# A convolution stage split in two: 11 batches ahead of the scans, 21 batches in slices beside them, with the band matrices kept in DRAM

## The chip, the core and the metric

The kernel runs on one core of one Trainium2 chip. The metric is the device time of one execution in microseconds. Engines are called by the profile's names: PE (TensorE matmul), PEld (its weight loads), DVE (VectorE), ACT (ScalarE), POOL (GpSimd), SP (the queue that issues DMAs).

## The reference, cut to what matters

The input is x, float32, 32 batches x 96 channels x 56 x 56. Two layers follow each other.

```python
# layer 0: ConvNeXt block
h = depthwise_conv7x7(x, conv_w, padding=3) + conv_b      # one 7x7 filter per channel
h = layernorm_over_channels(h) * ln_g + ln_b
h = gelu(h @ w1 + b1) @ w2 + b2
x1 = layer_scale * h + x

# layer 1: two Mamba blocks over the 3136 pixels of a batch as a sequence
seq = x1
for i in range(2):
    xs, z = split(layernorm(seq) @ in_w[i])               # 192 channels each
    xc = silu(causal_conv4(xs)); dt, Bm, Cm = split(xc @ xproj_w[i])
    delta = softplus(dt @ dt_w[i] + dt_b[i])
    h[t] = exp(delta*A) * h[t-1] + delta*xc * Bm          # 16 states per channel: a scan over t
    y = sum_states(h * Cm) + D * xc
    seq = seq + (y * silu(z)) @ out_w[i]
out = batchnorm(fuse(seq, pooled(x1))) + x1
```

Only the depthwise 7x7 convolution is placed differently by the change; the computation stays the same.

## The kernel before, in words

**The convolution stage.** The loop at L291 goes over 48 pairs of channels (`p`). A pair's image rows lie on the partitions: 2 channels x 56 rows = 112. The load at L293 brings all 32 batches of the pair into `xpad`, a tile padded by 3 columns on each side; its rows in DRAM are runs of 56 values, 224 bytes. Seven predicated copies on DVE (L298) write the taps of the pair into `band`, seven 112x112 band matrices, one for each horizontal tap. PE multiplies the seven matrices with seven shifted views of `xpad` (L307), 8 batches (448 columns) at a time, four groups per pair, 28 matmuls in all; a float32 matmul is two records in the profile. ACT adds the bias on the way out of PSUM (L311, tile `ct`), and the store at L314 writes the pair into `conv_d` in DRAM. `band` and `xpad` exist three times each. POOL has nothing to do here.

**The scan stages.** After that come 256 stages: 32 batches x 4 chunks of 784 pixels x 2 Mamba layers. The order of instructions is written out by hand (the manual schedule at L873): no scheduler moves anything, and each engine takes its instructions in the order of the Python code. A stage has 24 steps, six groups `j` of 32 channels times four groups `g` of states. A step has one scan on DVE (L798), ahead of it for most groups a product on DVE (L791), and after it one product on POOL (L802). For the groups j = 2 and j = 5 (`POOLED`) the first product is on POOL instead (L775): it reads the tile `us`, loaded by `load_u`, and its instructions lie at steps 0, 2, 4, 6 (j = 2) and 12, 14, 16, 18 (j = 5). `us` has two buffers. PE spreads the values of a group over 128 partitions for the product at L791 (`spread`, L764), at steps 3, 11, 15 and 23, and sums the states three steps behind the scan (`add_up`, matmuls L835 and L829). ACT computes the exponentials (L749) one or two steps ahead.

**The pieces around the scans.** Everything else is cut into pieces that carry a slot, a step number counted from the start of the stage (24 is the start of the next one, -10 is step 14 of the stage before). `run` calls a step's pieces in the order of the fraction. `prep` prepares the next Mamba stage: layer norm, the projections (L521), softplus (L586), and the loads of `bc` (L566), `d4` (L629) and `us` (L620). `post` at slot 7.5 projects the stage before (L682, L688). `block0` runs half a chunk of the ConvNeXt block of the next batch: it loads `cv` from `conv_d` (L379), and its pieces are `center` (PE, L343, slot 11.1), `square` (ACT, L348), `mean` (PE, L353), `root` (ACT, L359 and L360: logarithm and exponential) and `norm` at 14.1, a product on DVE (L405, output `hz`) that is called ahead of the scan of step 14; the MLP follows. The same step has the layer norm pieces of `prep`. PSUM banks `ps0` to `ps2` are single tiles that these pieces share.

**DMA.** All loads and stores go through the SP queue in the order of the code, apart from the output stores at the end. Each DMA takes one of eight completion semaphores in turn, and an issue waits for the DMA that had the same one before.

Of the kernel before, what the change touches and what calls it, by code (L numbers as in the profile page):

```python
# [30 lines left out]
F32 = mybir.dt.float32  # L34
I32 = mybir.dt.int32
AF = mybir.ActivationFunctionType
# [5 lines left out]
H = W = 56  # L42
L = H * W
C = 96
# [6 lines left out]
NCH = 4  # L51
CH = L // NCH
HC = CH // 2
ROWS = HC // W
# [6 lines left out]
def convnext_mamba_kernel(  # L61
# [31 lines left out]
    nc = tc.nc  # L93
    B = x.shape[0]

    dram = ctx.enter_context(tc.tile_pool(name="dram", bufs=1, space=DRAM))
    const = ctx.enter_context(tc.tile_pool(name="const", bufs=1))

    conv_d = dram.tile([C * H, B * W], F32, name="conv_d")
    stats_d = dram.tile([C, B * NCH, 12], F32, name="stats_d")  # L100
    x1_d = [dram.tile([C, L], F32, name=f"x1_d{b}", tag=f"x1_d{b}") for b in range(B)]
    o_d = [dram.tile([C, L], F32, name=f"o_d{b}", tag=f"o_d{b}") for b in range(B)]
# [83 lines left out]
    for i in range(2):  # L186
# [12 lines left out]
        if i == 1:  # L199

            d["res"] = fw1
            for q in range(NQ):
                ps = sups.tile([128, 512], F32, name="ps", tag="nps")
# [5 lines left out]
                ps = sups.tile([128, 512], F32, name="ps", tag="nps")  # L209
# [36 lines left out]


    R2 = 2 * H
    GB = min(8, B)
    with tc.tile_pool(name="cc", bufs=1) as cc, tc.tile_pool(name="cx", bufs=3) as cx, tc.tile_pool(  # L250
        name="cp", bufs=6, space=PSUM
    ) as cps:
        ones = cc.tile([R2, R2], F32, name="ones")
        nc.vector.memset(ones, 1.0)
        masks = []
        for dh in range(7):
            m = cc.tile([R2, R2], F32, name="m", tag="m", bufs=2)
# [13 lines left out]
            mi = cc.tile([R2, R2], I32, name=f"mi{dh}", tag=f"mi{dh}")  # L271
            nc.vector.tensor_copy(mi, m)
            masks.append(mi)
        cw = cc.tile([R2, C // 2, 49], F32, name="cw")
        cb = cc.tile([R2, C // 2], F32, name="cb")
        wv = conv_w.rearrange("(p two) k -> two p k", two=2)
        bv = conv_b.rearrange("(p two) k -> two p k", two=2)
        for j in range(2):
            nc.sync.dma_start(cw[j * H : (j + 1) * H], wv[j].partition_broadcast(H))
            nc.sync.dma_start(  # L280
                cb[j * H : (j + 1) * H].unsqueeze(2), bv[j].partition_broadcast(H)
            )
        bands, xpads = [], []
        for i in range(3):
            t = cc.tile([R2, 7, R2], F32, name=f"band{i}", tag=f"band{i}")
            nc.gpsimd.memset(t, 0.0)
            bands.append(t)
            t = cc.tile([R2, B, W + 6], F32, name=f"xpad{i}", tag=f"xpad{i}")
            nc.gpsimd.memset(t, 0.0)
            xpads.append(t)  # L290
        for p in range(C // 2):  # L291
            xp, T = xpads[p % 3], bands[p % 3]
            nc.sync.dma_start(  # L293
                xp[:, :, 3 : 3 + W],
                x[:, 2 * p : 2 * p + 2, :].rearrange("b c (h w) -> (c h) b w", w=W),
            )
            for dh in range(7):
                nc.vector.copy_predicated(  # L298
                    T,
                    masks[dh].unsqueeze(1).broadcast_to([R2, 7, R2]),  # L300
                    cw[:, p, dh * 7 : (dh + 1) * 7].unsqueeze(2).broadcast_to([R2, 7, R2]),
                )
            ct = cx.tile([R2, B * W], F32, name="ct")
            for gb in range(0, B, GB):
                ps = cps.tile([R2, GB * W], F32, name="ps")
                for dw in range(7):
                    nc.tensor.matmul(  # L307
                        ps, T[:, dw, :], xp[:, gb : gb + GB, dw : dw + W],
                        start=(dw == 0), stop=(dw == 6),
                    )  # L310
                nc.scalar.activation(  # L311
                    ct[:, gb * W : (gb + GB) * W], ps, AF.Identity, bias=cb[:, p : p + 1]
                )
            nc.sync.dma_start(conv_d[p * R2 : (p + 1) * R2, :], ct)  # L314


    with ExitStack() as main:
        wp = main.enter_context(tc.tile_pool(name="wp", bufs=2))
# [5 lines left out]
        def psum(k):  # L324

            return pp.tile([128, 512], F32, name="ps", tag=f"ps{k}", bufs=1)
# [17 lines left out]
            return ps  # L344

        def squared(ps):
            sq = wp.tile([C, HC], F32, name="sq", tag="sq", bufs=3)
            nc.scalar.activation(sq, ps[0:C, 0:HC], AF.Square)  # L348
            return sq

# [20 lines left out]
        def block0(b, c, s):  # L371
            k = c * 2 + s
            v = {}

            def load():
                if k == 0:
                    batch_sums[b] = wp.tile([C, NCH * 2], F32, name="sums", tag="sums", bufs=2)
                v["cv"] = wp.tile([C, ROWS, W], F32, name="cv", tag="cv", bufs=1)
                nc.sync.dma_start(  # L379
                    v["cv"],  # L380
                    conv_d.rearrange("(c h) w -> c h w", h=H)[
                        :, k * ROWS : (k + 1) * ROWS, b * W : (b + 1) * W
                    ],
                )

# [68 lines left out]
            def fuse():  # L454
# [3 lines left out]
                nc.scalar.activation(fb, ps[0:C, 0:1], AF.Identity, bias=fusb)  # L458
                batch_bias[b] = fb

            last = [(21.5, total), (33.3, pool), (34.3, fuse)] if k == 2 * NCH - 1 else []
            return last + [
                (-6, load), (2, load_x), (11.1, center), (12.1, square), (12.4, mean),
                (12.8, root), (14.1, True, norm), (15.6, up), (15.9, gelu), (17.3, down),
                (18.3, residual),
            ]


# [6 lines left out]
        def prep(S):  # L475

            i, b, c = S.i, S.b, S.c
            d = lay[i]
            v = {}
# [135 lines left out]

            def load_u(k):
                def piece():
                    t = wp.tile([128, CH], F32, name="us", tag="us", bufs=2)
                    for s in range(4):
                        nc.sync.dma_start(t[32 * s : 32 * s + 32], v["uu"][k])  # L620
                    S.us[POOLED[k]] = t

                return piece

            def load_d4(j):
                def piece():
# [14 lines left out]
            t = (-7.6, -7.5, -6.5, -6, 0, 0.1, 1, 2.3, 3.1, 3.4, 4)  # L641
# [7 lines left out]
            elif S is stages[3]:  # L649
# [17 lines left out]
                (max(18.3, t[10] + 3.1), store_u(0)), (25.2, product(2)), (26.3, store_u(1)),  # L667
                (max(17, t[10] + 2), load_d4(0)), (max(18, t[10] + 3), load_d4(1)),
                (max(20, t[10] + 3.2), load_u(0)), (23, load_d4(2)),
                (26, load_d4(3)), (28.9, load_u(1)), (30, load_d4(4)), (35, load_d4(5)),  # L670
            ]

        def post(S):
# [55 lines left out]
        for i, b, c in order:  # L729
            S = Stage()  # L730
            S.i, S.b, S.c, S.d, S.da, S.e = i, b, c, lay[i], {}, {}
            stages.append(S)
        halfs = [(b, c, s) for b in range(1, B) for c in range(NCH) for s in range(2)]

        def wide():
# [107 lines left out]
        def put(m, pieces):  # L843
            for slot, *piece in pieces:
                where = slots if len(piece) == 1 else within
                where.setdefault(m * NSTEP + math.floor(slot), []).append((slot % 1, piece[-1]))
# [14 lines left out]
        for m, S in enumerate(stages):  # L861
            if m:
                put(m, post(stages[m - 1]))
            for j in POOLED:
                put(m, [(NG * (j - 2) + 2 * g, pooled(m, j, g)) for g in range(NG)])
            if 2 <= m < len(halfs) + 2:
                put(m, block0(*halfs[m - 2]))
            if m + 1 < len(stages):
                put(m, prep(stages[m + 1]))
        put(len(stages), post(stages[-1]))  # L870
# [116 lines left out]
```

## Time and profile before

| what | value |
|---|---|
| median of 3 runs | 18194.72 us (18187.29 to 18194.83) |
| profiled execution, device time | 18182.61 us |
| its span, first to last instruction | 18180.9 us |
| convolution stage, first to last matmul of L307 | 97.8 to 1120.4 us |
| batch 0 of the ConvNeXt block and the first preparation | 1120 to about 1307 us |
| scan stages, first to last scan of L798 | 1307 to 17804 us, 64.4 us a stage (16497 / 256) |
| final batch norm and output | to the end |

The profiled execution lies 12 us below the median. The spans in the table are starts of instructions in the trace.

How to read the page: busy time of an engine is the time in which at least one of its instructions runs. In a list of groups, a line gives the code line, the engine, the operation, the tiles written and read, their shapes, the count, the busy time in us, the mean duration in ns, and the idle time ahead of them with what ended it. In the timeline a line gives start, duration, engine, line and operation; merged instructions carry a count. PEclk is the clock granted to PE as a share of full speed.

### The profile page before, as it was taken

Reading aid. Unit: us, or ns where it says so; the run is one execution under the profiler, and the core shown is the slowest. Engines: PE = TensorE matmul, PEld = TensorE weight load, DVE = VectorE, ACT = ScalarE, POOL = GpSimd, SP = SyncE. Lnnn points to the kernel's source line nnn. Section 1 sums busy time; section 2 is a strip of 40 time slices with the busy share of each in tenths; the row PEclk is TensorE's granted clock in tenths of the full one; section 3 lists DMA queues with packets and bytes.
Section 4 is the critical chain, followed back from the end, with each engine's and each line's share of the span. In section 5 each row is a group of like instructions: output and inputs, shape, how many; then the busy total and the mean of one; then the engine's idle time right before and its main releaser. Section 6 shows DMA issues by size and latency. Waiting matters only on the chain. (4 is left out here: it accounts for less than half of the span.)

```text
span 18180.9 us, 209835 instructions
## 1 busy us (share of the span) xinstructions
PE 15482.2 (85%) x65304; PEld 5247.5 (29%) x65304; DVE 16188.3 (89%) x12591; ACT 11251.4 (62%) x17431; POOL 15631.6 (86%) x8993
## 2 busy tenths in 40 slices
PE   8988888888888888888888888888888888888871
PEld 3432222222222222222222222222222222222220
DVE  3329999999999999999999999999999999999994
ACT  0136666666666666666666666666666666666652
POOL 0019999999999999999999999999999999999991
PEclk9989999999999999999999999999999999999985
DMA  3324555555555555555555555555555555555548
GB/s 69 75 70 120 128 126 126 127 126 126 124 127 125 129 126 129 124 129 125 126 126 126 127 126 127 124 127 124 128 125 129 126 129 124 129 125 127 126 110 271
DMA packets 1358198, 2279.26 MB, mean 125 GB/s; under 512 B 619974, under 2 KB 751346, under 8 KB 1357076
## 3 DMA queue, kind: packets, MB, share of 16 engines
q1 hardware_dynamic: 1349908, 2227.31, 49.6%
q10 hardware_dynamic: 7168, 38.54, 0.6%
q8 instruction: 515, 8.44, 0.2%
q14 instruction: 607, 4.97, 0.1%
HBM read 1878.92 MB, written 385.94 MB: 125 GB/s over the span
## 5 line engine op out<-in xcount | busy, mean ns | idle before, releaser
L802 POOL TENSOR_TENSOR da<-h,bc 128x784 f32<-128x784 f32 x6144 | 11268.8, 1855 | 901.2 <-DVE h L798 860.7
L798 DVE TENSOR_TENSOR_SCAN h<-da,st,w 128x784 f32<-128x784 f32 x3072 | 5663.4, 1844 | 312.7 <-ACT st L809 9.1
L835 PE MATMUL y<-da,ssum 128*32 128x392 f32 x24576 | 5053.7, 534 | 943.7 <-POOL da L802 936.9
L791 DVE TENSOR_TENSOR w<-w,bc 128x784 f32<-128x784 f32 x4096 | 3997.2, 976 | 207.3 <-PE w L764 23.3
L775 POOL TENSOR_TENSOR da<-us,bc 128x784 f32<-128x784 f32 x2048 | 3810.3, 1861 | 1.0 <-DMA us<-uu 0.9
L749 ACT ACTIVATE da<-d,A 128x784 f32<-128x784 f32 x4096 | 3739.9, 941 | 46.6 <-DMA d<-dd 22.6
L749 ACT ACTIVATE w<-d,A 128x784 f32<-128x784 f32 x2048 | 1880.4, 918 | 2770.1 <-DVE h L798 2422.5
L798 DVE TENSOR_TENSOR_SCAN h<-w,st,da 128x784 f32<-128x784 f32 x1536 | 2712.4, 1827 | 6.4 <-ACT w L749 5.3
L835 PEld LDWEIGHTS y<-da,ssum 128*32 128x32 f32 x24576 | 1104.6, 114 | 4550.1 <-issue 2276.5
L521 PE MATMUL ps<-hn,wx 97*64 97x392 f32 x12288 | 2259.2, 502 | 7.4 <-DVE hn L509 7.4
L798 DVE TENSOR_TENSOR_SCAN h<-da,w 128x784 f32<-128x784 f32 x1024 | 1826.3, 1783 | 108.2 <-ACT st L809 5.2
L600 POOL TENSOR_TENSOR u<-dl,xc 128x392 f32<-128x392 f32 x768 | 785.3, 1023 | 1222.0 <-ACT dl L586 1222.0
L764 PE MATMUL w<-u,sel 64*128 64x392 f32 x4096 | 1111.7, 624 | 779.5 <-DVE h L798 779.2
L521 PEld LDWEIGHTS ps<-hn,wx 97*64 97x64 f32 x12288 | 791.3, 136 | 1417.6 <-issue 1097.7
L829 PE MATMUL y<-xc,D 128*128 128x392 f32 x1536 | 838.3, 634 | 348.9 <-DVE z L816 347.5
L307 PE MATMUL ps<-xpad,band 112*112 112x448 f32 x2688 | 1022.6, 542 | 47.3 <-DMA xpad<-in_x 47.3
L339 ACT ACT_TABLE_LOAD x759 | 973.8, 1283 | 14.4 <-PEq L974 0.8
L298 DVE COPY_PREDICATED band<-mi,cw 112x784 f32<-112x784 int32 x336 | 347.7, 1039 | 653.1 <-PE ps L307 630.6
L798 DVE TENSOR_TENSOR_SCAN h<-w,da 128x784 f32<-128x784 f32 x512 | 872.1, 1765 | 0.0
L359 ACT ACTIVATE ps<-ps,eps_c 96x392 f32<-96x392 f32 x768 | 422.5, 550 | 703.8 <-PE ps L353 703.7
L764 PEld LDWEIGHTS w<-u,sel 64*128 64x128 f32 x4096 | 347.6, 208 | 1502.7 <-DVE h L798 1408.7
L578 PE MATMUL ps<-dbl,dtw 6*64 6x392 f32 x3072 | 689.5, 512 | 100.3 <-ACT dbl L556 100.3
(108 smaller groups left out, 13972.0 us busy)
## 6 DMA issues: line engine op xcount, KB each, us to landing
bc<-bd SPq DMA_DIRECT2D x4096, 196.0 KB, 5.4
d<-dd SPq DMA_DIRECT2D x6144, 98.0 KB, 2.3
us<-uu SPq DMA_DIRECT2D x2048, 98.0 KB, 2.4
dd<-dl SPq DMA_DIRECT2D x512, 294.0 KB, 3.7
uu<-u SPq DMA_DIRECT2D x1024, 49.0 KB, 1.6
xpad<-in_x SPq DMA_DIRECT2D x48, 784.0 KB, 6.1
conv_d<-ct SPq DMA_DIRECT2D x48, 784.0 KB, 7.1
cv<-conv_d SPq DMA_DIRECT2D x256, 147.0 KB, 2.5
```

Of the source, the lines that this page charges most:

```text
L307: nc.tensor.matmul(ps, T[:, dw, :], xp[:, gb : gb + GB, dw : dw + W], start=(dw == 0), stop=(dw == 6),)
L339: nc.scalar.preload_act_table_set("natural_log_exp_and_others")
L521: nc.tensor.matmul(v["x", q][rows(a), 0:HC], weights[:, k, 64 * q : 64 * q + 64], v["hn"][:, o : o + HC], start=(k == 0), stop=(k == last),)
L600: nc.gpsimd.tensor_tensor(S.u[:, q], v["dl"][:, q], S.xc[:, q], ALU.mult)
L749: nc.scalar.activation(e, S.d4[j], AF.Exp, scale=S.d["A"][:, j, g : g + 1])
L764: nc.tensor.matmul(S.u4[:, 512 * a : 512 * a + HC], sel[rows(a), j % 2, :], S.u[rows(a), j // 2, :], start=True, stop=True,)
L775: nc.gpsimd.tensor_tensor(t, S.us[j], S.bcs[g][:, 0, :], ALU.mult)
L791: nc.vector.tensor_tensor(halves(db), S.u4.rearrange("p (a b) -> p a b", a=2)[:, :, 0:HC], halves(S.bcs[g][:, 0, :]), ALU.mult,)
L798: nc.vector.tensor_tensor_scan(ring[:, g, :], S.e.pop((j, g)), db, 0.0 if c == 0 else d["st"][:, j, g : g + 1], ALU.mult, ALU.add,)
L802: nc.gpsimd.tensor_tensor(da, ring[:, g, :], S.bcs[g][:, 1, :], ALU.mult)
L829: nc.tensor.matmul(S.y[:, 0:HC], S.d["D"][:, q, :], S.xc[:, q, :], start=True, stop=False)
L835: nc.tensor.matmul(S.y[r0 : r0 + 32, 0:HC], ssum, da[:, tok(a)], start=False, stop=(g == NG - 1),)
```

## The change

The convolution stage does only the first 11 batches, two groups of 6 and 5 batches per pair instead of four of 8. Each pair's seven band matrices are stored to DRAM (`band_d`). The other 21 batches form three groups of seven; a new set of pieces, `conv`, does two channels of seven batches in each of the scan stages 2 to 145 (3 x 48 = 144): it loads band matrices and image at slot -10, issues seven matmuls of 112 x 392 on PE at slots 7.7 to 10.4 into the bank `ps2`, and at 11.05 moves the result through ACT into a tile of the tag `sq` and stores it. `conv_d` becomes four tensors, one per group. `us` goes from two buffers to one and its second load from slot 28.9 to 32.9; `sq` grows from 96 to 112 partitions; `center` of `block0` goes from 11.1 to 11.3, and its `pool` and `fuse` from 33.3 and 34.3 to 29.9 and 30.9.

```diff
+    NB = 7
+    b0 = B - 3 * NB if B > 3 * NB else B
+    groups = [(0, b0)] + [(b, b + NB) for b in range(b0, B, NB)]
+    conv_d = [dram.tile([C * H, (hi - lo) * W], F32, ...) for lo, hi in groups]
+    band_d = dram.tile([C // 2, 2 * H, 7 * 2 * H], F32, name="band_d")
...
-    GB = min(8, B)
+    GB = (b0 + 1) // 2
+    cb = const.tile([R2, C // 2], F32, name="cb")
...
         for p in range(C // 2):
             xp, T = xpads[p % 3], bands[p % 3]
-                x[:, 2 * p : 2 * p + 2, :].rearrange("b c (h w) -> (c h) b w", w=W),
+                x[0:b0, 2 * p : 2 * p + 2, :].rearrange("b c (h w) -> (c h) b w", w=W),
...
+            nc.sync.dma_start(band_d[p], T.rearrange("p k n -> p (k n)"))
-            for gb in range(0, B, GB):
+            for lo in range(0, b0, GB):
+                n = min(GB, b0 - lo)
...
-            nc.sync.dma_start(conv_d[p * R2 : (p + 1) * R2, :], ct)
+            nc.sync.dma_start(conv_d[0][p * R2 : (p + 1) * R2, :], ct)
...
-            sq = wp.tile([C, HC], F32, name="sq", tag="sq", bufs=3)
+            sq = wp.tile([R2, HC], F32, name="sq", tag="sq", bufs=3)[0:C]
...
-            last = [(21.5, total), (33.3, pool), (34.3, fuse)] if k == 2 * NCH - 1 else []
+            last = [(21.5, total), (29.9, pool), (30.9, fuse)] if k == 2 * NCH - 1 else []
-                (-6, load), (2, load_x), (11.1, center), (12.1, square), (12.4, mean),
+                (-6, load), (2, load_x), (11.3, center), (12.1, square), (12.4, mean),
...
+        xpad = wp.tile([R2, NB, W + 6], F32, name="xpad", tag="xpad", bufs=1)
+        nc.vector.memset(xpad, 0.0)
+        def conv(g, p):
+            lo, hi = groups[g]
+            def load():
+                v["band"] = wp.tile([R2, 7, R2], F32, name="band", tag="band", bufs=1)
+                nc.sync.dma_start(v["band"].rearrange("p k n -> p (k n)"), band_d[p])
+                nc.sync.dma_start(xpad[:, :, 3 : 3 + W],
+                    x[lo:hi, 2 * p : 2 * p + 2, :].rearrange("b c (h w) -> (c h) b w", w=W))
+            def taps_(dws):
+                def piece():
+                    if dws[0] == 0:
+                        v["ps"] = psum(2)
+                    for dw in dws:
+                        nc.tensor.matmul(v["ps"][0:R2, 0 : NB * W], v["band"][:, dw, :],
+                            xpad[:, :, dw : dw + W], start=(dw == 0), stop=(dw == 6))
+                return piece
+            def store():
+                t = wp.tile([R2, HC], F32, name="sq", tag="sq", bufs=3)
+                nc.scalar.activation(t[:, 0 : NB * W], v["ps"][0:R2, 0 : NB * W],
+                    AF.Identity, bias=cb[:, p : p + 1])
+                nc.sync.dma_start(conv_d[g][p * R2 : (p + 1) * R2, :], t[:, 0 : NB * W])
+            return [
+                (-10, load), (7.7, taps_((0,))), (8.2, taps_((1,))), (8.6, taps_((2,))),
+                (9.2, taps_((3,))), (9.6, taps_((4,))), (10.2, taps_((5,))), (10.4, taps_((6,))),
+                (11.05, store),
+            ]
...
-                    t = wp.tile([128, CH], F32, name="us", tag="us", bufs=2)
+                    t = wp.tile([128, CH], F32, name="us", tag="us", bufs=1)
...
-                (26, load_d4(3)), (28.9, load_u(1)), (30, load_d4(4)), (35, load_d4(5)),
+                (26, load_d4(3)), (32.9, load_u(1)), (30, load_d4(4)), (35, load_d4(5)),
...
+        convs = [(g, p) for g in range(1, len(groups)) for p in range(C // 2)]
...
+            if 2 <= m < len(convs) + 2:
+                put(m, conv(*convs[m - 2]))
```

More of the change, by code (lines that the diff above doesn't have):

```diff
@@ L97, in convnext_mamba_kernel @@
     const = ctx.enter_context(tc.tile_pool(name="const", bufs=1))
-    conv_d = dram.tile([C * H, B * W], F32, name="conv_d")
+    NB = 7
+    b0 = B - 3 * NB if B > 3 * NB else B
+    groups = [(0, b0)] + [(b, b + NB) for b in range(b0, B, NB)]
+    conv_d = [
+        dram.tile([C * H, (hi - lo) * W], F32, name=f"conv_d{lo}", tag=f"conv_d{lo}")
+        for lo, hi in groups
+    ]
+    band_d = dram.tile([C // 2, 2 * H, 7 * 2 * H], F32, name="band_d")
     stats_d = dram.tile([C, B * NCH, 12], F32, name="stats_d")
@@ L274, in convnext_mamba_kernel @@
         cw = cc.tile([R2, C // 2, 49], F32, name="cw")
-        cb = cc.tile([R2, C // 2], F32, name="cb")
         wv = conv_w.rearrange("(p two) k -> two p k", two=2)
@@ L287, in convnext_mamba_kernel @@
             bands.append(t)
-            t = cc.tile([R2, B, W + 6], F32, name=f"xpad{i}", tag=f"xpad{i}")
+            t = cc.tile([R2, b0, W + 6], F32, name=f"xpad{i}", tag=f"xpad{i}")
             nc.gpsimd.memset(t, 0.0)
@@ L302, in convnext_mamba_kernel @@
                 )
-            ct = cx.tile([R2, B * W], F32, name="ct")
-            for gb in range(0, B, GB):
+            nc.sync.dma_start(band_d[p], T.rearrange("p k n -> p (k n)"))
+            ct = cx.tile([R2, b0 * W], F32, name="ct")
+            for lo in range(0, b0, GB):
+                n = min(GB, b0 - lo)
                 ps = cps.tile([R2, GB * W], F32, name="ps")
@@ L307, in convnext_mamba_kernel @@
                     nc.tensor.matmul(
-                        ps, T[:, dw, :], xp[:, gb : gb + GB, dw : dw + W],
+                        ps[:, 0 : n * W], T[:, dw, :], xp[:, lo : lo + n, dw : dw + W],
                         start=(dw == 0), stop=(dw == 6),
@@ L311, in convnext_mamba_kernel @@
                 nc.scalar.activation(
-                    ct[:, gb * W : (gb + GB) * W], ps, AF.Identity, bias=cb[:, p : p + 1]
+                    ct[:, lo * W : (lo + n) * W], ps[:, 0 : n * W], AF.Identity,
+                    bias=cb[:, p : p + 1],
                 )
-            nc.sync.dma_start(conv_d[p * R2 : (p + 1) * R2, :], ct)
+            nc.sync.dma_start(conv_d[0][p * R2 : (p + 1) * R2, :], ct)
     with ExitStack() as main:
@@ L378, in load @@
                 v["cv"] = wp.tile([C, ROWS, W], F32, name="cv", tag="cv", bufs=1)
+                g = 0 if b < b0 else 1 + (b - b0) // NB
+                at = (b - groups[g][0]) * W
                 nc.sync.dma_start(
                     v["cv"],
-                    conv_d.rearrange("(c h) w -> c h w", h=H)[
-                        :, k * ROWS : (k + 1) * ROWS, b * W : (b + 1) * W
+                    conv_d[g].rearrange("(c h) w -> c h w", h=H)[
+                        :, k * ROWS : (k + 1) * ROWS, at : at + W
                     ],
@@ L459, in fuse @@
                 batch_bias[b] = fb
-            last = [(21.5, total), (33.3, pool), (34.3, fuse)] if k == 2 * NCH - 1 else []
+            last = [(21.5, total), (29.9, pool), (30.9, fuse)] if k == 2 * NCH - 1 else []
             return last + [
-                (-6, load), (2, load_x), (11.1, center), (12.1, square), (12.4, mean),
+                (-6, load), (2, load_x), (11.3, center), (12.1, square), (12.4, mean),
                 (12.8, root), (14.1, True, norm), (15.6, up), (15.9, gelu), (17.3, down),
                 (18.3, residual),
+            ]
+        xpad = wp.tile([R2, NB, W + 6], F32, name="xpad", tag="xpad", bufs=1)
+        nc.vector.memset(xpad, 0.0)
+        def conv(g, p):
+            lo, hi = groups[g]
+            v = {}
+            def load():
+                v["band"] = wp.tile([R2, 7, R2], F32, name="band", tag="band", bufs=1)
+                nc.sync.dma_start(v["band"].rearrange("p k n -> p (k n)"), band_d[p])
+                nc.sync.dma_start(
+                    xpad[:, :, 3 : 3 + W],
+                    x[lo:hi, 2 * p : 2 * p + 2, :].rearrange("b c (h w) -> (c h) b w", w=W),
+                )
+            def taps_(dws):
[3 more added lines that the diff above has]
+                    for dw in dws:
+                        nc.tensor.matmul(
+                            v["ps"][0:R2, 0 : NB * W], v["band"][:, dw, :],
+                            xpad[:, :, dw : dw + W], start=(dw == 0), stop=(dw == 6),
+                        )
+                return piece
+            def store():
+                t = wp.tile([R2, HC], F32, name="sq", tag="sq", bufs=3)
+                nc.scalar.activation(
+                    t[:, 0 : NB * W], v["ps"][0:R2, 0 : NB * W], AF.Identity, bias=cb[:, p : p + 1]
+                )
+                nc.sync.dma_start(conv_d[g][p * R2 : (p + 1) * R2, :], t[:, 0 : NB * W])
[3 more added lines that the diff above has]
+                (11.05, store),
             ]
```

## The prediction

> **What bounds the kernel now.** I read the page's busy table first, then its 40 slices, the windows by stage, the groups, and at last the timelines of one stage.
>
> ```profile
> PE 15482.2 (85%) x65304; PEld 5247.5 (29%) x65304; DVE 16188.3 (89%) x12591; ACT 11251.4 (62%) x17431; POOL 15631.6 (86%) x8993
> ...
> PE   8988888888888888888888888888888888888871
> ...
> DVE  3329999999999999999999999999999999999994
> ```
>
> Three engines near 90% of the whole say little; the slices say that DVE is only 20 to 30% busy in the first 1,350 us. The windows (time, then busy us per engine, granted clock, DMA share, GB/s) split that:
>
> ```profile
> core 0: us, PE busy (x) PEld busy (x) DVE busy (x) ACT busy (x) POOL busy (x), PEclk, DMA share, GB/s
> 98.00:1120.00 1022.00, 1022.00 (x2688) 470.79 (x2688) 327.74 (x315) 120.97 (x191) 0.00 (x0) 1.00 0.33 74
> 1120.00:1290.00 170.00, 116.89 (x250) 45.90 (x248) 5.74 (x11) 80.53 (x118) 1.98 (x2) 0.67 0.13 35
> 1290.00:17790.00 16500.00, 14323.22 (x62294) 4723.59 (x62294) 15681.52 (x12104) 10932.12 (x17042) 15601.27 (x8949) 0.92 0.51 126
> ```
>
> The convolution stage is bound by PE alone (1022 of 1022 us); the scan stages by DVE, 95% busy, the rest nearly all turnarounds of about 0.1 us. In 5000 to 12000 us, 109 stages, DVE has one wait that counts (engine, line, waited for: us in all, times, longest):
>
> ```profile
> DVE hz L405 <- ACT ps L360: 73.1, 68, 2.3
> ```
>
> That is 0.67 us a stage. PE's 87% there isn't 87% of its capacity. Around steps 8 to 12 of a stage, the timeline and two windows show:
>
> ```profile
> 5009.15 2.22 PE L688 MATMUL ps<-z,ow 64*96 64x392 f32 x12
> 5011.30 1.51 PE L835 MATMUL y<-da,ssum 128*32 128x392 f32 x8
> 5015.56 0.85 PE L835 MATMUL y<-da,ssum 128*32 128x392 f32 x4 [2.75 <-POOL da L802]
> 5018.11 1.68 PE L764 MATMUL w<-u,sel 64*128 64x392 f32 x4 [1.70 <-DVE h L798]
> 5019.72 1.62 PE L343 MATMUL ps<-cv,center_m 96*96 96x392 f32 x2
> 5021.14 2.82 PE L343 MATMUL ps<-seq,center_m 96*96 96x392 f32 x4
> ```
>
> ```profile
> 5012.00:5018.00 6.00, 1.66 (x10) 0.24 (x8) 6.00 (x5) 4.10 (x6) 6.00 (x4) 0.93 1.03 233
> 5018.00:5024.00 6.00, 5.89 (x11) 2.62 (x12) 5.86 (x6) 3.46 (x9) 5.47 (x4) 0.50 0.64 140
> ```
>
> PE idles 2.75 + 1.70 = 4.45 us during steps 8 to 11, then runs at half clock: the spread L764 takes 1.68 us where another of the same stage takes 0.93, a centring matmul 1.4 to 1.6 instead of 0.7. That cold stretch is what makes `hz` late.
>
> [...]
>
> **The change, part by part.**
>
> *Convolution stage, PE.* A matmul of 448 columns costs 1022 / 1344 = 0.760 us; a pair has 28, 21.3 us. A pair now has 7 x 336 and 7 x 280 columns; by columns 7 x 0.760 x 616/448 = 7.3 us[...]. *DVE* has as many copies as before and becomes co-limiter:
>
> ```profile
> L298 DVE COPY_PREDICATED band<-mi,cw 112x784 f32<-112x784 int32 x336 | 347.7, 1039 | 653.1 <-PE ps L307 630.6
> 1014.16 7.49 DVE L298 COPY_PREDICATED band<-mi,cw 112x784 f32<-112x784 int32 x7 [13.78 <-PE ps L307]
> ```
>
> The first line's idle time, 653 us waiting for PE, goes; 7.5 us a pair stays (second line). The first three bands are built before PE starts, as now; the first image, 11/32 as large, lands some 5 us sooner (three issues take SP 24.05 us, 8 each; 11/32 of 8 is 2.8): PE starts near 92.5, finishes pair 0 near 102; DVE builds 45 more bands in 338 us, to 440; the last pair ends at **447** instead of 1120.4. **Saved: 673 us.** The rest of this stage hides: ACT two moves of under 0.63 us a pair; the band's store (343 KB) and the smaller image and result make 881 KB in 7.5 us, 118 GB/s, under the 271 GB/s that the page's last slice shows; SP's band store waits for DVE, and behind it stand the result's store and the next image's load, which has two pairs (15 us) in hand for a landing of 6.1 us. If these don't hide I allow 1 us a pair, +50; no gain beyond PE's 7.3 is possible.
>
> *Scan stages, PE.* Seven taps of 392 columns in each of 144 stages. At full clock the nearest rows start 0.66 us apart (L410, L429), so 4.6 us[...]; at half clock 9.2. They stand between `post` and the spread of step 11, in the 4.45 us of idling. From the end of `post` (5011.3): taps 4.9, three pairs of L835 2.3, giving 5018.5; spread 0.93 warm, 5019.4; DVE's product needs it at 5019.9. On this stage nothing is lost. Reading all stages so, `post` ends 21.4 us after step 0 in the median, but 22.9 in a quarter of them, where the spread comes 1 to 2 us late: 0.35 us on average, 144 x 0.35 = **+50 us**, with bounds of 0 (PE catches up earlier, being warm) and 1.6 us in every stage, +230.
>
> *Afterwards.* PE is warm: centring ends near 5021.6 instead of 5023.9. The four users of the three `sq` buffers make the third square wait for the first mean (0.5 us on ACT before the logarithm). Even so `hz` has its input near 5026.6, against 5028.1 before. Its wait goes: 144 x 0.7 = **-100 us** (bounds: that, and 0 if the squares are late); next late is the spread.
>
> *ACT, DVE, POOL.* ACT: one move of 0.5 us, in the place of idling of 0.91 us; behind it are one exponential, needed a step or two later, and the squares. The centring of `cv` waits for this move through `ps2`; it stands after two other centrings. DVE: one memset, 0.4 us once. POOL: nothing. `pool`/`fuse`: moved 31 times, 0.25 us pieces on PE and ACT, hidden.
>
> *DMA.* Per stage 343 KB of bands, 172 KB of image and as much result: 686 KB beside 126 GB/s x 64.4 us = 8.1 MB, share 0.51 to 0.55, needed some 18 steps later. Hidden; if not, it shows as late `d` or `bc`, priced at 0 to 1 us a stage; I take 0.
>
> *One `us` buffer.*
>
> ```profile
> 5011.86 1.85 POOL L775 TENSOR_TENSOR da<-us,bc 128x784 f32<-128x784 f32 x1
> 5025.06 1.84 POOL L775 TENSOR_TENSOR da<-us,bc 128x784 f32<-128x784 f32 x1
> us<-uu SPq DMA_DIRECT2D x2048, 98.0 KB, 2.4
> ```
>
> The second load now waits for the reader that ends at 5013.7 (it was issued at 5005.4) and is needed at 5025.06: 11.4 us for four issues (1.7 to 3 us) and a landing of 2.4, at most 5.1. Behind it in SP's queue wait eight `bc`, four `d` and the `conv_d` store. `bc` is for the next stage, some 40 us off; `d` is read from step 19 on, some 20 us off. The first load waits 1.5 us longer at step 20 and is needed 11 us later. Cost 0; with this cover gone, POOL and so DVE would wait.
>
> *Sum.* 18182.6 (profiled execution) - 673 + 50 - 100 = 17460; the median lies 12 us above that execution, so **17470**.
>
> **The rivals.**
> *A, the slices cost some of what they save.* Taps run partly cold or wait on `ps2` or DMA; stages grow by 0.5 to 2.5 us, 70 to 360 us: about 17650. For it: in a quarter of the stages the margin is negative already. Against: PE idles 13% of 64.4 = 8.4 us a stage, so 3.5 stay, and it waits for DVE at the next spread (0.74 us at 5030.45).
> *B, slower: the taps run at half clock.* If PE comes to them cold, 7 x 1.31 = 9.2 us, the spread is 4 to 5 us late and DVE stands still at step 12 of every slice. The point is 673 / 144 = 4.7 us a stage; 5.5 would give 18310. Against: PE is busy and warm from 5007 to 5012, and the taps remove the idling that cools it.
> *C, the convolution stage is bound otherwise*, by band stores or DVE's predicated copies at 9 to 10 us a pair: about 17570.
> *D, the work isn't moved or overlapped at all*: the built order has 672 matmuls in the first stage and seven in each of 144, so no.
>
> **How the numbers follow.** Forecast 0.67, A 0.17, C 0.11, B 0.04, D 0.01. Range 17370 to 17690: below, no late spread and a smoother stage; above, most of A and C. 0.2% (36 us) is about what a measurement can tell from no change. Faster 0.95, same 0.01, slower 0.04.
>
> **What would show it.** Right: last matmul of the convolution stage near 447 us, DVE full there; seven taps per stage with clock 1.00 at steps 8 to 13; no `hz` wait in stages 2 to 145 and it back in later ones; a small wait of L791 on the spread L764. Wrong: stages 2 to 145 longer than 65.4 us, DVE waiting there on PE or DMA, or over 8.5 us a pair in the first stage.

## The result, and the profile after

The changed kernel takes 17504.03 us (median of 4 runs, 17503.2 to 17516.66) beside 18194.78 for the kernel before: ratio 0.9623, 95% interval 0.9606 to 0.9639. The forecast was 17470, range 17370 to 17690. The profiled execution took 17504.21 us, its span is 17502.5, 678.4 us shorter than the span before.

First the page after: the busy line, then PE, DVE and the granted clock in the 40 slices.

```profile
PE 15285.5 (87%) x65976; PEld 5191.4 (30%) x65976; DVE 16171.5 (92%) x12592; ACT 11224.1 (64%) x17479; POOL 15632.4 (89%) x8993
...
PE   7799999999999999999999988888888888888880
...
DVE  7499999999999999999999999999999999999994
...
PEclk9799999999999999999999999999999999999985
```

DVE's row began with 332 and now begins with 74: the stretch in which it was mostly waiting is gone. PE's row reads 9 up to about the 23rd slice, where the slices of convolution end (10006 us), and 8 after it. The windows by stage (time; busy us and count of PE, PEld, DVE, ACT, POOL; granted clock, DMA share, GB/s) say where the time went:

```profile
core 0: us, PE busy (x) PEld busy (x) DVE busy (x) ACT busy (x) POOL busy (x), PEclk, DMA share, GB/s
0.00:98.00 98.00, 7.84 (x24) 3.27 (x24) 20.71 (x65) 3.21 (x9) 8.88 (x33) 1.00 0.27 39
98.00:450.00 352.00, 344.88 (x1311) 230.42 (x1312) 337.08 (x331) 48.19 (x93) 0.00 (x0) 1.00 0.45 120
450.00:620.00 170.00, 119.25 (x275) 49.20 (x273) 6.15 (x12) 77.36 (x113) 0.01 (x1) 0.68 0.11 29
620.00:9900.00 9280.00, 8547.94 (x37131) 2848.91 (x37132) 8807.84 (x6811) 6240.57 (x9783) 8777.20 (x5034) 0.96 0.57 137
9900.00:17110.00 7210.00, 6252.77 (x27188) 2055.91 (x27184) 6858.28 (x5291) 4740.19 (x7411) 6826.64 (x3917) 0.92 0.51 125
```

The convolution stage now fills PE (345 of 352 us) and DVE (337) at once. The stages with slices (620 to 9900) have PE 92% busy at clock 0.96, those without 87% at 0.92. Measured from scan to scan in the traces:

| stretch, us | before | after | difference |
|---|---|---|---|
| start to the first scan (the convolution stage lies here) | 1307.5 | 641.8 | -665.7 |
| stages 2 to 145, first scan to first scan | 9262.9 | 9256.8 | -6.1 |
| stages 146 to 249, likewise | 6691.6 | 6688.6 | -3.0 |
| after the last scan | 376.5 | 374.2 | -2.3 |

The small remainder of the 678 us lies in the first two and the last six stages. So 1008 matmuls were put into 144 stages without lengthening them (64.3 us each, as before). The forecast had them 50 us shorter in all. What DVE waits for in the stages with slices, and then in later ones (engine, line, waited for: us in all, times, longest):

```profile
DVE w L847 <- PE w L820: 126.5, 115, 4.8
```

```profile
DVE hz L419 <- ACT ps L372: 73.8, 69, 2.3
```

The `hz` wait is absent from the first window and there again in the later stages. In its place, in the stages with slices, the product L847 waits for the spread L820. At step 12 of stages 2 to 145 that comes to 105 us, 0.73 a stage, counted without the 0.1 us by which this product always starts after the scan ahead of it; the rest is that 0.1 us, other steps and the first two stages. All waits for the spread and for `hz` below are counted in this way.

One stage that shows it, number 46: PE's timeline (start, duration, line, operation; in brackets the idle time ahead) around the cold stretch and around the taps, and three windows over it.

```profile
3619.64 2.17 PE L603 MATMUL ps<-xc,xp 64*38 64x392 f32 x12
3621.74 0.93 PE L820 MATMUL w<-u,sel 64*128 64x392 f32 x4
3623.08 3.07 PE L633 MATMUL ps<-dbl,dtw 6*64 6x392 f32 x12 [0.42 <-ACT dbl L611]
3626.09 1.68 PE L885 MATMUL y<-xc,D 128*128 128x392 f32 x2
3627.69 4.86 PE L891 MATMUL y<-da,ssum 128*32 128x392 f32 x20
...
3633.97 2.22 PE L743 MATMUL ps<-z,ow 64*96 64x392 f32 x12
3636.12 0.91 PE L503 MATMUL ps<-xpad,band 112*112 112x392 f32 x2
...
3642.34 1.58 PE L503 MATMUL ps<-xpad,band 112*112 112x392 f32 x4
3643.85 0.93 PE L820 MATMUL w<-u,sel 64*128 64x392 f32 x4
```

```profile
3621.20:3624.60 3.40, 2.98 (x17) 1.19 (x15) 3.16 (x3) 3.33 (x8) 3.40 (x4) 1.00 0.20 56
3624.60:3631.40 6.80, 6.80 (x25) 1.79 (x22) 6.46 (x7) 5.07 (x7) 6.80 (x5) 0.53 0.41 99
3631.40:3646.00 14.60, 14.60 (x58) 5.27 (x53) 12.68 (x9) 7.89 (x13) 14.47 (x8) 0.99 0.59 150
```

The taps L503 run at full speed: 7.3 us from the start of the first to the start of the last, the `add_up` pairs between them included, in this stage and in all others (5th to 95th percentile 7.31 to 7.32). But PE comes to them late. From 3624.6 to 3631.4, that is in steps 4 and 5, it ran at half clock (0.53): L885 took 1.68 us where it takes 0.82 later in the stage. `post` ended 23 us after step 0, and the spread, ready at 3644.8, let the scan of step 12 begin only at 3646.20, 1.69 us late. The taps keep PE busy without a gap from there on, so the delay can't be caught up before step 12.

The stages as a whole show the same. Sorted by how long the clock was halved in steps 2 to 8:

| halved clock in steps 2 to 8 | stages | end of `post` after step 0 | wait for the spread, mean | in all |
|---|---|---|---|---|
| none | 46 | 21.1 us | 0.11 us | 5.0 us |
| 3.4 us | 68 | 21.6 us | 0.50 us | 34.3 us |
| 6.8 us or more | 30 | 23.2 us | 2.19 us | 65.7 us |

What halves the clock there? In the 3.40 us ahead of it (3621.2 to 3624.6) PE is busy for 2.98 us. But from 3623.08 on, the last 1.5 us of that window, it runs L633, the projection of `dbl` with `dtw`, whose matmuls have 6 rows (`6*64` in its line). Whether that is the cause, the experiments have to say.

The start of the first stage is the other deviation. SP's queue after (start, time held, line, transfer):

```profile
48.48 12.92 SPq L289 DMA_DIRECT2D cb<-in_conv_b  x2
61.73 24.20 SPq L288 DMA_DIRECT2D cw<-in_conv_w  x2
85.97 6.69 SPq L302 DMA_DIRECT2D xpad<-in_x  x3
```

Before, one half of `cw` went first, at 51.60, and both tiles were through at 74.5; now both `cb` loads stand ahead of `cw`, which is through at 85.9. The images, smaller, do take only 6.69 us instead of 24.05. DVE's first copy, which needs `cw`, moves from 76.5 to 92.9, and PE's first matmul from 97.8 to 105.1.

### The profile page after: what moved, and what is told of

Read it like the earlier page. It is cut to its first block, busy times and chain, and to the rows that moved or that the text cites. A ratio compares the mean times of both kernels' runs of the same rounds, so it can differ in the third digit from the quotient of the medians.

```text
span 17502.5 us, 212206 instructions
## 1 busy us (share of the span) xinstructions
PE 15285.5 (87%) x65976; PEld 5191.4 (30%) x65976; DVE 16171.5 (92%) x12592; ACT 11224.1 (64%) x17479; POOL 15632.4 (89%) x8993
## 5 line engine op out<-in xcount | busy, mean ns | idle before, releaser
L847 DVE TENSOR_TENSOR w<-w,bc 128x784 f32<-128x784 f32 x4096 | 3996.0, 976 | 311.0 <-PE w L820 139.5
L820 PE MATMUL w<-u,sel 64*128 64x392 f32 x4096 | 1032.9, 583 | 719.0 <-DVE h L854 719.0
L885 PE MATMUL y<-xc,D 128*128 128x392 f32 x1536 | 796.8, 605 | 306.9 <-DVE z L872 305.2
L360 ACT ACTIVATE sq<-ps 96x392 f32<-96x392 f32 x768 | 340.6, 490 | 827.2 <-PE ps L355 529.7
L503 PE MATMUL ps<-xpad,band 112*112 112x392 f32 x2016 | 816.1, 520 | 0.0
L633 PE MATMUL ps<-dbl,dtw 6*64 6x392 f32 x3072 | 684.2, 509 | 100.3 <-ACT dbl L611 100.3
L820 PEld LDWEIGHTS w<-u,sel 64*128 64x128 f32 x4096 | 327.2, 196 | 1424.7 <-DVE h L854 1262.4
L865 ACT COPY st<-h 128x2 f32<-128x2 f32 x2304 | 417.5, 181 | 426.3 <-DVE h L854 424.9
```

Of the source, the lines that this page charges most:

```text
L503: nc.tensor.matmul(v["ps"][0:R2, 0 : NB * W], v["band"][:, dw, :], xpad[:, :, dw : dw + W], start=(dw == 0), stop=(dw == 6),)
L820: nc.tensor.matmul(S.u4[:, 512 * a : 512 * a + HC], sel[rows(a), j % 2, :], S.u[rows(a), j // 2, :], start=True, stop=True,)
L847: nc.vector.tensor_tensor(halves(db), S.u4.rearrange("p (a b) -> p a b", a=2)[:, :, 0:HC], halves(S.bcs[g][:, 0, :]), ALU.mult,)
L885: nc.tensor.matmul(S.y[:, 0:HC], S.d["D"][:, q, :], S.xc[:, q, :], start=True, stop=False)
```

## The experiments

The theory: (1) the stage saving is real and is limited by PE and DVE together; (2) the missing 50 us are the late spread, and it is late because PE's clock is halved at steps 4 and 5 after the 6-row matmuls; (3) the slices remove the `hz` wait by keeping PE warm at steps 8 to 11. The rivals: the taps are simply too much work for that place, whatever the clock; or the `hz` wait went for another reason than warmth. Times below are compared as the difference to the kernel before, run on the same chip. For the change itself it is -690.7 us, and -685.6 when it was run again (17510.95, ratio 0.9622, 0.9608 to 0.9636):

> The changed kernel as it is, on the chip of e9, as a measure for the small differences between chips: 17504 within 15; e9 below it by 110 to 150 us if its theory holds.

All edits are to the changed kernel unless said otherwise.

**Rows of the `dt` matmul, 6 to 38.** The same product with zero rows added (NX is 38); nothing else of the schedule moves.

```diff
-        dtw = const.tile([DTR, DIN], F32, name=f"dtw{i}", tag=f"dtw{i}")
-        nc.sync.dma_start(dtw, dt_w[i])
+        dtw = const.tile([NX, DIN], F32, name=f"dtw{i}", tag=f"dtw{i}")
+        nc.vector.memset(dtw, 0.0)
+        nc.sync.dma_start(dtw[0:DTR], dt_w[i])
...
-                            v["dbl"][0:DTR, tok(a)], start=True, stop=True,
+                            v["dbl"][0:NX, tok(a)], start=True, stop=True,
```

> The changed kernel, with the delta projection multiplying all 38 rows of dbl by weights that are zero beyond the first 6, in place of 6 rows; the result is the same. Theory ([...]PE is at half clock in steps 4 and 5, post ends late and the spread of step 11 after it): granted clock in steps 4 and 5 of the slices from 0.71 and 0.82 to 0.95 or more, DVE's waits for L820 in stages 2 to 145 from about 105 us to 30 or less, time 17504 - 80 = 17425 (17400 to 17450). Rival 1 (the number of rows doesn't matter to the clock): clock as it was, 17504 within 15. Rival 2 (the clock warms, but the spread is late for the taps' length alone): clock 0.95 or more and still 17504 within 15.

Measured: 17471.54 us, ratio 0.9600 (0.9586 to 0.9614), difference -728.1. The clock in steps 4 and 5, taken from the start of one scan to the start of the next, rose from 0.74 and 0.79 (the expectations say 0.71 and 0.82) to 0.84 and 0.91, the wait for the spread fell from 105 to 53 us, stages 2 to 145 from 9256.8 to 9216.4. The direction is the theory's, the size half of it.

**128 rows.** `dbl` becomes one tile of 128 partitions, zeroed once, `dtw` 128 rows, zero beyond the sixth.

```diff
+        dblt = wp.tile([128, CH], F32, name="dbl", tag="dbl", bufs=1)
+        nc.vector.memset(dblt, 0.0)
...
-                            v["dbl"][0:DTR, tok(a)], start=True, stop=True,
+                            v["dbl"][:, tok(a)], start=True, stop=True,
```

> The changed kernel with the delta projection multiplying 128 rows (6 of dbl that count, the others by zero weights); the result is the same. Theory ([...]38 rows of 128 removed half of the cold stretches, 128 remove nearly all): clock in steps 4 and 5 of the slices from 0.71 and 0.82 to 0.97 or more, spread wait in stages 2 to 145 from 105 us to 20 or less, time 17504 - 80 = 17424 (17405 to 17445). Rival (the cold stretches there follow the short weight columns or the wait for dbl, not the rows, and 38 rows helped by chance of phase): clock at most 0.9, time as with 38 rows, 17472 within 15.

Measured: 17456.86 us, ratio 0.9599 (0.9583 to 0.9615), difference -725.0. This is stage 46 again, the same three places: the `dt` matmuls and the one after them, then two windows, those 3.4 and 6.8 us long.

```profile
3609.35 2.57 PE L637 MATMUL ps<-dbl,dtw 128*64 128x392 f32 x12 [0.42 <-ACT dbl L615]
3611.85 0.93 PE L889 MATMUL y<-xc,D 128*128 128x392 f32 x2
```

```profile
3607.40:3610.80 3.40, 2.98 (x19) 1.14 (x15) 3.16 (x3) 3.33 (x8) 3.40 (x4) 1.00 0.19 52
3610.80:3617.60 6.80, 6.43 (x32) 2.10 (x29) 6.46 (x7) 5.14 (x7) 6.80 (x4) 1.00 0.40 98
```

PE is busy just as long in the first window (2.98 us) as it was with 6 rows, and the clock after it is 1.00 instead of 0.53. In 143 of 144 stages the clock is never halved in steps 2 to 8; the wait for the spread is 20.7 us instead of 105, with all seven taps in place, and stages 2 to 145 take 9188.9 us, 68 less. (The wait shrank by 84 us; 15 of them came back at step 20, where DVE now waits for the sum `y`.) The 64 weight columns and the wait for `dbl` (0.42 us) are as they were. That settles (2), and both rivals with it, the one of this run and the one of too many taps: at the same busy time it was the number of rows that made the difference here. The 20.7 us that stay have another cause, which is open. The whole gained only half of the 68 us, less than the range expected: stages 146 to 249, which have no slices, grew by 14 us (their `hz` wait went from 0.64 to 0.76 us a stage), and the end after the last scan by 10.

**One tap of seven.**

```diff
-                            xpad[:, :, dw : dw + W], start=(dw == 0), stop=(dw == 6),
+                            xpad[:, :, dw : dw + W], start=True, stop=True,
...
-                (-10, load), (7.7, taps_((0,))), (8.2, taps_((1,))), (8.6, taps_((2,))),
-                (9.2, taps_((3,))), (9.6, taps_((4,))), (10.2, taps_((5,))), (10.4, taps_((6,))),
+                (-10, load), (7.7, taps_((0,))),
```

> The changed kernel with one matmul of the seven left in each slice (the other six taps of the 21 batches are left out; loads, the move by ACT and the stores stay). Theory (the taps remove the wait for hz because they keep PE from idling and cooling, and their length is what makes the spread late): spread wait from 105 us to under 10, PE idles again at steps 8 to 11, clock in steps 11 and 12 back to about 0.6, hz wait back to 0.65 us a stage, 94 us in 144 stages: 17495 (17475 to 17515). Rival (the wait for hz went because the centring pieces or the square buffers were moved, not by the clock): hz wait stays away, 17504 - 105 = 17400.

Measured: 17537.06 us, ratio 0.9637 (0.962 to 0.9653), difference -662.6: with six taps fewer in each stage the kernel is some 25 us slower, and above the range expected. DVE's waits over 640 to 9920 us:

```profile
DVE hz L419 <- ACT ps L372: 118.5, 104, 2.8
```

The late spread at step 12 is gone (0.6 us in all) and the `hz` wait is back, at 0.77 us a stage; the clock at steps 10 to 12 is 0.83, 0.62, 0.70 instead of 1.00. So the six taps do cost the stage their late spread, 105 us, but they spare it the `hz` wait, 110 us, and it is work on PE at this place that keeps that wait away: the moved centring pieces and the square buffers are still as the change has them.

**Unread matmuls in the later stages.** Four matmuls of 112 x 392 whose result nobody reads, in stages 146 to 249.

```diff
+        def idle_taps(at):
...
+                    nc.tensor.matmul(
+                        v["ps"][0:R2, 0 : NB * W], lay[0]["D"][0:R2, 0, 0:R2],
+                        xpad[:, :, 3 : 3 + W], start=(k == 0), stop=(k == len(at) - 1),
+                    )
...
+            if len(convs) + 2 <= m < len(halfs) + 2:
+                put(m, idle_taps([7.7, 8.2, 8.6, 9.2]))
```

> The changed kernel with four matmuls of 112 x 392 without a reader added at the taps' places in stages 146 to 249, where there are no slices; no loads, no ACT work, no stores with them. Theory (PE work in the idle steps keeps the clock and so hz in time; four fit without making the spread late): hz wait in these stages from 68 us to under 10, spread wait under 15, clock in steps 10 to 12 from 0.56 to 0.75 up to 1.0, 17504 - 60 = 17444 (17425 to 17460). Rival (hz comes in time in the slices for another reason, and added matmuls only cost): 17504 to 17560.

Measured: 17440.28 us, ratio 0.9584 (0.9569 to 0.9598), difference -759.4. Those stages went from 6688.6 to 6620.3 us, 68 less, with clock 1.00, 0.97 and 0.99 at steps 10 to 12 (without them 0.79, 0.57 and 0.66) and no `hz` wait. DVE's first two waits from 9900 to 16550 us:

```profile
DVE z L888 <- PE y L907: 7.1, 5, 2.5
DVE w L863 <- PE w L836: 5.7, 6, 1.7
```

Adding work to PE made the kernel faster (-759.4 us beside -690.7), with no load, move or store beside it: (3) holds from both sides.

**`cb` behind the first image.** Two attempts to mend the late start. The first only moved the two `cb` loads in the code to behind the first image:

> The changed kernel with the filter load cw issued ahead of the bias load cb, which goes behind the first image loads. Theory (the first band waits for cw behind cb's 4-byte pieces, 92.9 us against 76.5 before): first predicated copy at about 70 us, first matmul at about 85 instead of 105, everything after it 20 us earlier, 17484 (17475 to 17495). Rival (the queue's backlog sets the landing whatever the order): first matmul stays at 100 us or later, 17504 within 10.

Measured: 17516.0 us, ratio 0.9625 (0.9611 to 0.964). It missed its object: the built kernel still issued `cb` first (at 48.55), and the first copy stayed at 92.7. It says nothing about the theory. The second loads `cb` into a tile of the convolution stage and lets ACT copy it:

```diff
-            nc.sync.dma_start(cb[j * H : (j + 1) * H].unsqueeze(2), bv[j].partition_broadcast(H))
...
+            if p == 0:
+                cb0 = cc.tile([R2, C // 2], F32, name="cb0")
+                for j in range(2):
+                    nc.sync.dma_start(
+                        cb0[j * H : (j + 1) * H].unsqueeze(2), bv[j].partition_broadcast(H))
+                nc.scalar.copy(cb, cb0)
```

> The changed kernel with the bias loaded through a tile of the convolution stage and copied by ACT, so that in SP's queue the filter load cw stands ahead of cb and the first image ahead of it too (in e3 the built order still had cb first, so it changed nothing). Theory: cw is issued from 48.5 instead of 61.7, first predicated copy near 80 instead of 92.9, first matmul near 90 instead of 105.1, all later stages 13 to 16 us earlier: 17490 (17482 to 17497). Rival (cb's small pieces delay the images instead and PE starts as late): 17504 within 8.

Measured: 17497.05 us, ratio 0.9622 (0.9608 to 0.9637), difference -684.8: no gain that can be told. The first copy came at 61.8 us and the first matmul at 74.05, 31 us earlier, but the timeline of PE shows the next wait:

```profile
74.05 10.23 PE L322 MATMUL ps<-xpad,band 112*112 112x336 f32 x28 [24.40 <-DVE band L304]
96.86 28.43 PE L322 MATMUL ps<-xpad,band 112*112 112x336 f32 x101 [12.59 <-DMA xpad<-in_x]
```

PE waits 12.59 us for the second image, which stands in SP's queue behind `cb`; DVE waits 16.67 us for the first store of a band. The first scan is 16 us earlier and the stretch after the last scan 7 us longer. So the queue order explains the late start, and moving one transfer only moves the wait.

**One `us` buffer alone**, in the kernel before:

```diff
-                    t = wp.tile([128, CH], F32, name="us", tag="us", bufs=2)
+                    t = wp.tile([128, CH], F32, name="us", tag="us", bufs=1)
...
-                (26, load_d4(3)), (28.9, load_u(1)), (30, load_d4(4)), (35, load_d4(5)),
+                (26, load_d4(3)), (32.9, load_u(1)), (30, load_d4(4)), (35, load_d4(5)),
```

> The kernel before with two parts of the change alone: one us buffer and its second load at slot 32.9. Theory (11 us in hand hide the later load): same as before within 12 us, POOL's wait for us under 5 us in all. Rival (SP's queue, held by this load, makes bc or d late, and the changed kernel's scans pay for it): 50 us or more above before.

Measured: 18181.57 us (12 runs) beside 18181.85, ratio 1.0 (0.9991 to 1.0008). What POOL waited for `us` in the whole run:

```profile
POOL da L775 <- DMA us<-uu: 1.1, 2, 0.9
```

The second buffer was worth nothing, as forecast.

**The parts together.** 128 rows, the unread matmuls and the later `cb` in one kernel:

> The changed kernel with three edits together: 128 rows in the delta projection, four unread matmuls at the taps' places in stages 146 to 249, and the load order of e7. Theory (three separate waits, so the gains add): 17504 - 80 - 64 - 14 = 17346 (17325 to 17375). Rival (removing one exposes another on DVE or POOL, and they don't add): 17400 or more.

Measured: 17363.06 us, ratio 0.9548 (0.9533 to 0.9562), difference -818.8. Stages 2 to 145 take 9188.0 us and 146 to 249 6628.5: the two gains, 69 and 60 us, stand in different stages and add up.

**Seven batches ahead instead of eleven.** With 128 rows and unread matmuls; the other 25 batches in four groups, slices in stages 2 to 193, unread matmuls in 194 to 249. The expectation leaves the load order of `cb` out, but the kernel that ran has it, so it is to be compared with the one above. Of its edit against that one, the lines that matter (the slices' widths follow):

```diff
-    b0 = B - 3 * NB if B > 3 * NB else B
-    groups = [(0, b0)] + [(b, b + NB) for b in range(b0, B, NB)]
+    b0 = 7
+    groups = [(0, 7), (7, 14), (14, 20), (20, 26), (26, 32)]
```

> The kernel of e8 without its load order, with 7 batches ahead (two groups of 4 and 3 per pair) and 25 in four groups of 7, 6, 6 and 6 in stages 2 to 193; the unread matmuls only in stages 194 to 249. It moves 36% of what is left of PE's work in the convolution stage into the scans. Theory (DVE's seven copies a pair, 7.36 us, set that stage as much as PE did, and PE's work beside the scans is free once it is warm): first scan at 640 us as before the move, time 17504 - 80 - 58 = 17370 within 20, PE idle by a third in the convolution stage. Rival (PE set that stage and DVE only kept pace): 4.9 us a pair, first scan near 520, time near 17250.

Measured: 17287.72 us, ratio 0.9501 (0.9485 to 0.9517), difference -908.8, the best of all. The first scan is at 576.1 us; in the kernel above it was at 627.4. So 51 us are the stage's; the rest of the difference lies in the scan stages and the end, and what made it is not shown. Its convolution stage by windows, and a stretch of copies beside one of the changed kernel (the count ends the line):

```profile
105.00:360.00 255.00, 194.86 (x1113) 176.42 (x1112) 255.00 (x279) 33.50 (x79) 0.00 (x0) 1.00 0.39 111
```

```profile
199.26 26.72 DVE L305 COPY_PREDICATED band<-mi,cw 112x784 f32<-112x784 int32 x29
```

```profile
194.80 40.95 DVE L307 COPY_PREDICATED band<-mi,cw 112x784 f32<-112x784 int32 x39
```

DVE is the only bound here, 255 of 255 us. But it takes 26.72 / 29 = 0.92 us a copy, 6.45 a pair; in the changed kernel it is 40.95 / 39 = 1.05, 7.4 a pair. If the copies' pace had been fixed, fewer batches ahead would have brought nothing in this stage. So the theory had the bound right and its price wrong, and the rival had the bound wrong. The pace changed with the order of the copies: the built program of this version fills two bands in turn, the one of the changed kernel fills each band to its end first. The last section shows what that does.

## Why the prediction was right, and where it missed

**The bound.** Right. The convolution stage was PE's alone, and its time left the total: 665.7 us to the first scan, of 673 foreseen.

**7.3 us a pair.** Right, and as a reading too: two limits within 1% of each other. PE takes 7.32 us from pair to pair (7.37 on average, with one wait at the start), DVE 7.36, and DVE waits for PE 1.7 us in all. It goes at its own pace: it begins the fourth pair 0.04 us after PE has freed the band, and later and later, the last one 1.9 us after. What the prediction did not see is that 7.5 us for seven copies is the price of this order of copies, not of DVE; in turn on two bands they took 6.45 (seven batches ahead).

**"PE starts near 92.5".** Wrong, 105.1. The step counted the smaller images, rightly, and not that moving `cb` out of the stage's pool changes where its loads stand in SP's queue. The last pair ended near 458.8 instead of 447; the batch after it and the first preparation were 4 us shorter, so the miss is 7 us.

**Seven taps at full clock, rival B out.** Right: 7.3 us, clock 1.00 at steps 8 to 13.

**The `hz` wait gone, -100.** Right: 0.64 us a stage at step 14 before, 0.00 after, 92 us; the whole step got 111 us shorter over the 144 stages. The reason, a warm PE, was tested both ways. In how the cold comes about the prediction was too quick: its 4.45 us of idling are two gaps, 2.75 and 1.70 us, with 0.85 us of matmuls between them. The profile has the clock halved from 5017.1 to 5023.9 us, that is from before the end of the second gap (5018.11) on, and PE was busy 0.85 us in the 3.40 us ahead of that (first of the two windows). How much idling it takes is not shown.

```profile
5013.70:5017.10 3.40, 0.85 (x4) 0.14 (x4) 3.40 (x3) 2.37 (x5) 3.40 (x3) 1.00 1.03 220
5017.10:5023.90 6.80, 5.79 (x11) 2.52 (x12) 6.66 (x6) 4.35 (x9) 6.27 (x5) 0.50 0.70 153
```

**The late spread, +50.** The term that was mis-sized: 105 us, 0.73 a stage instead of 0.35. I estimated it from the scatter of `post` in the kernel before, with too much room behind it: in the changed kernel the spread is late by what the end of `post` exceeds 21.3 us after step 0 (20.5 in some stages). With 21.3 the same scatter of the kernel before gives 0.53 us a stage; the rest is that `post` ends 0.1 us later on average, and those stages with less room. The scatter's cause lies ahead of `post`, in the halved clock at steps 4 and 5, which the change doesn't touch (0.76 and 0.79 there before, 0.74 and 0.79 after), and the taps take the idle time in which PE used to catch up.

**The sum.** -6 us in the stages with slices instead of -50 makes 44 us; the start makes 7; the later stages and the end gave 5 back. 17460 + 44 + 7 - 5 = 17506, measured 17504.21. Step by step the -6 has no rest: step 12 grew by 105 us over the 144 stages, step 14 shrank by 111, and all others together changed by less than 1. Rival A, slices that cost 0.5 us or more a stage, did not come true, nor did C: 7.37 us a pair, not 9 to 10.

**The rest.** DMA, ACT and the `us` buffer cost nothing: share 0.57 where 0.55 was foreseen, and of DVE's waits on a transfer one of 8.6 us counts in the stages with slices. Of these only the `us` buffer was tested alone.

## What to carry to other kernels

Work for an engine that idles was nearly free here, in stages that another engine bounds and at the steps where PE had idled: 1008 matmuls in 144 stages, 64.3 us a stage with and without them. The unread matmuls even paid, 68 us in 104 stages, because they kept PE's clock up (1.00, 0.97 and 0.99 at steps 10 to 12 instead of 0.79, 0.57 and 0.66). Look up what the clock was at the moment your insertion starts, not only during it: a delay made earlier, until then absorbed by idling, came out at the next deadline once the idle time was filled, here 105 us at step 12. And when a tile moves to another pool, or a stage changes its size, read the order of the built kernel again from the start: here it moved a load in the DMA queue (first copy at 92.9 us instead of 76.5), and in the last version it made DVE's copies faster (0.92 us instead of 1.05).

## What the hardware did that I had not expected

**After matmuls of few rows the clock was halved.** In stage 46 PE was busy 2.98 of 3.40 us, half of that with matmuls of 6 rows, and over the 6.8 us after it the clock was 0.53; with the same busy time and 128 rows it was 1.00. Over stages 2 to 145 the clock in steps 4 and 5 was 0.74 and 0.79 with 6 rows, 0.84 and 0.91 with 38, and 1.00 and 1.00 with 128. So PE's busy time did not tell which clock followed; by what rule the rows matter is not shown. The rows that were added hold zero weights. Padding with zero rows cost PE no time: 2.57 us for the twelve records in stage 46, where the 6 rows took 3.07, partly at half clock.

**A copy into the tile of the copy ahead waited for its end.** From start to start a predicated copy took 0.91 to 0.95 us in some places and 1.05 to 1.09 in others. The order in which the built program has the copies tells which. Where a copy and the next one write different bands, the next started 0.10 to 0.13 us before the first had ended. Where they write the same band, the next one started 0.03 us after its end. So it is in the kernel before and the changed kernel, in 276 of 276 such pairs of each, and for every copy into another band that waits for nothing else (14 and 58). In the version with seven batches ahead, with two bands in turn, it is 0.92 us. PE's work does not decide it: these two stretches of the kernel before lie ahead of its first matmul of this stage (busy us and count of PE, PEld, DVE). In the first the copies go to two bands in turn, in the second all to the third band:

```profile
76.50:89.10 12.60, 0.00 (x0) 0.00 (x0) 12.60 (x14) 0.00 (x0) 0.00 (x0) 1.00 0.15 16
89.20:96.50 7.30, 0.00 (x0) 0.00 (x0) 7.09 (x8) 0.00 (x0) 0.00 (x0) 1.00 0.47 93
```

DVE has no gap in the first, 0.91 us a copy, and a gap of 0.03 us ahead of each copy in the second, 1.06 us a copy.
